# Two graph attention layers on one Trainium2 core: another order of the last pairs' work, and the bias product with its pieces side by side

## The chip, the core and the metric

The kernel runs on one core of one Trainium2 chip. A core has five engines that run side by side, each its own instructions in their order: TensorE (PE; its weight loads are the row PEld), VectorE (DVE), ScalarE (ACT), GpSimd (POOL) and SyncE (SP), which issues transfers. The metric is the device time of one execution in microseconds (us), lower is better.

## The reference

The input x has 64 graphs of 256 nodes with 512 features, float32, and one 256 x 256 adjacency matrix `adj` for all graphs. Two layers follow each other, each with a normalization, a ReLU and a residual:

```python
h = jnp.maximum(_layernorm(x, axis=-1), 0.0)
x = x + _L0_gnn_ref(h, adj, Wq, bq, Wk, bk, Wv, bv, Wo, bo)
h = jnp.maximum(_layernorm(x, axis=-1), 0.0)
x = x + _L1_gnn_ref(h, W, a, beta, adj)

# _L0_gnn_ref: 8 heads of 64
q, k, v = (h @ Wq + bq), (h @ Wk + bk), (h @ Wv + bv)        # as (b, n, 8, 64)
scores = einsum('bqhd,bkhd->bhqk', q, k) / 8 + (1 - adj) * -1e9
out = einsum('bhqk,bkhd->bqhd', softmax(scores), v)
return out @ Wo + bo

# _L1_gnn_ref
g = h @ W
e = leaky_relu((g @ a1)[:, :, None] + (g @ a2)[:, None, :], 0.2) * adj
return elu(softmax(e, axis=2) @ g + beta * g)
```

## The kernel before

The 64 graphs are worked on in 32 pairs. Each product with a weight matrix is one 2 x 2 block product: the two graphs of the pair are the rows, the two halves of the features the columns. It is done with seven block products in place of eight (a Strassen-like scheme), at the price of sums of blocks. A `Unit` is such a product for one pair: `UnitQK`, `UnitV`, `UnitO` (Wo) and `UnitW` (W of layer 1). Its method `p(i)` issues block product i on TensorE into the unit's PSUM banks `a`, `c` or `b`; for i = 1, 6, 7 ScalarE then copies bank `a` to SBUF (`u1`, `u2`, `u3`, line L278). `put11`, `put22`, `put21`, `put12` make the four result blocks from banks and copies. The blocks that go in are combined by `combine_31` (blocks 7 and 5), `combine_2` (block 6, L294) and `combine_4` (block 3, L298).

The order of every engine but SyncE is exactly the order in which the program is written (`tc.manual_schedule`), so where a call stands decides what an instruction queues behind. The stages of a pair p are: projections, scores and softmax (L416, L420, L421), `values` (L434, L443, L445), Wo with the residual (`UnitO`, L484 and L488), normalization of the result y (`y_stats`, `scales`, `normal`, L514), `node_sums` (L520; it is called by `y_sums`), `gat_scores` (L170, L530, L532), `gat_exp` (L537), `divide_1` (L542, L544), `gat_t` (four transposes on TensorE, L553, and a copy on ScalarE, L554), `z_graph` (L566, with copies on ScalarE, L569), and `UnitW`, whose blocks go through `elu` (ScalarE: L594, L595; VectorE: L599) and `finish` (POOL: L604; transfer out on SyncE: L605). Different pairs are in different stages at once. `first_half` and `second_half` do the steady state; `last` and `end` write out the order of the last two pairs, p - 1 and p. In `end`, `uv` is the `UnitW` of pair p - 2, `uw` that of pair p - 1 and then of pair p, `uo` the `UnitO` of pair p.

- `residual` (L466, L467) fetches a block of x and adds `bo2` on POOL; `o_blocks` makes two combined blocks on POOL (L459).
- `project_b` makes `bo2` = bo - 1 + bv Wo once, at the start. Its `part(0)` (called as `shift(0)`) spreads bv over 128 columns for each of four pieces of 128 rows (L191), `part(1)` multiplies them with Wo, adding the pieces up in PSUM (L197), and adds the result to `bo2` (L199). Its -1 belongs to elu.
- `in_range` (L726 to L728) looks on VectorE whether all softmax sums were in range; `count` adds the answer over partitions with one TensorE product (L733) and writes a flag, which decides whether a slow general version runs. With these inputs it does not.
- `p_34` does the last unit's products 3 and 4, and L632 and L636 add up the block of product 3 in its own bank; `put21_finish` makes the very last block in two halves (L645 to L651).

Tiles come from pools with a fixed number of buffers per tag (`BUFS`), and all PSUM tiles from 8 banks.

Of the kernel before, what the change touches and what calls it, by code (L numbers as in the profile page):

```python
# [11 lines left out]
ALU = mybir.AluOpType  # L12
# [11 lines left out]
def kernel(ctx: ExitStack, tc: tile.TileContext, x, adj, wq, bq, wk, bk, wv, bv, wo, bo, w, a, beta, out):  # L24
# [30 lines left out]
    def sb(shape, tag, name, bufs=2):  # L55
        return pools["sb"].tile(shape, F32, tag=tag, name=name, bufs=bufs)
# [3 lines left out]
    def blk(tag, name):  # L60

        return sb([P, 2, N], tag, name, BUFS[tag])
# [4 lines left out]
    def two(ps):  # L67
        return ps.rearrange("p (j n) -> p j n", j=2)
# [103 lines left out]
    def project_b():  # L172


        WO, b12, fetch, sums = weight("wo", wo, True)
        fetch(*range(4))
        nc.sync.dma_start(bo2, bo.partition_broadcast(P))
        bvc = sb([P, DC], "bvc", "bvc", 1)
        with nc.allow_non_contiguous_dma(reason="a bias, once"):
            bv_v = bv.rearrange("(q i s d) -> i d q s", q=2, i=4, s=2, d=HH)  # L180
            for i in range(4):
                for q in range(2):
                    nc.sync.dma_start(bvc[i * HH:(i + 1) * HH, 2 * q:2 * q + 2], bv_v[i, :, q, :])
        cbs = []

        def part(n):
            if n == 0:
                for c in range(DC):
                    if c % 2 == 0:
                        cbs.append(sb([P, 2, P], "rec", f"bvb_{c}"))  # L190
                    nc.vector.tensor_scalar(cbs[-1][:, c % 2, :], ones, bvc[:, c:c + 1], None, ALU.mult)  # L191
            else:
                ps = bank("pbo")
                for c in range(DC):
                    for f in range(2):
                        b = ((WO[1], b12), (WO[2], WO[3]))[c // 2][f]
                        nc.tensor.matmul(ps[:, f * N:(f + 1) * N], cbs[c // 2][:, c % 2, :], b[:, c % 2, :],  # L197
                                         start=(c == 0 and f == 0), stop=(c == DC - 1), skip_group_check=True)
                nc.vector.scalar_tensor_tensor(bo2, bo2, -1.0, ps, op0=ALU.add, op1=ALU.add)  # L199

        return WO, part, sums
# [79 lines left out]
        s = A[key] = {"name": name}  # L281
        return s

    def combine_31(s, a21, a22, tag="set"):

        s["tag"] = tag
        s[7] = blk(tag, f"s3_{s['name']}")
        a21(s[7], ALU.subtract, s[1])
        s[5] = s.pop("a21")
        a22(s[5], ALU.add, s[5])  # L290

# [158 lines left out]
            nc.vector.tensor_tensor(OT[b, q], two(ps), rec.unsqueeze(1).to_broadcast([P, 2, N]), ALU.mult)  # L450


    def o_blocks(p, tag="set"):
        s = blocks(("o", p), f"o{p}")
        for i, (gi, q) in zip(BLOCK, ((0, 0), (0, 1), (1, 0), (1, 1))):
            s[i] = OT.pop((2 * p + gi, q))

        def of(src):
            return lambda dst, op, other: nc.gpsimd.tensor_tensor(dst, src, other, op)  # L459

        combine_31(s, of(s["a21"]), of(s[4]), tag)

    def residual(p, gi, fh, tag):
        g = 2 * p + gi
# [119 lines left out]
    class UnitW(Unit):  # L584
# [41 lines left out]
            nc.vector.tensor_tensor(two(self.b), two(self.b), self.u2, ALU.add)  # L626
            self.elu(0, 1, two(self.b))

        def p_34(self):

            t = self.u2
            nc.vector.tensor_tensor(t, two(self.b), t, ALU.add)  # L632
            e = bank(f"{self.name}_p3")
            self.mm(3, e, True)
            self.p(4)
            nc.vector.tensor_tensor(two(e), two(e), t, ALU.add)  # L636
            self.elu(0, 1, two(e))

        def put21_finish(self):

            g = 2 * self.pair + 1
            y = Y.pop((g, 0))
            v, m, o = (blk("v", f"{c}_{g}_0") for c in "vmo")
            for t in range(NT):
                nc.vector.tensor_copy(v[:, t, :], self.a[:, t * N:(t + 1) * N])  # L645
                nc.scalar.activation(m[:, t, :], v[:, t, :], AF.Exp)
            for t in range(NT):
                nc.vector.scalar_tensor_tensor(o[:, t, :], v[:, t, :], 0.0, y[:, t, :], op0=ALU.max, op1=ALU.add)
            for t in range(NT):
                nc.vector.scalar_tensor_tensor(o[:, t, :], m[:, t, :], 1.0, o[:, t, :], op0=ALU.min, op1=ALU.add)  # L650
                nc.sync.dma_start(out[g, t * P:(t + 1) * P, :N], o[:, t, :])  # L651


    def products(u, *which):
# [59 lines left out]
    def combine_24(s):  # L714
        combine_2(s)
        combine_4(s)
# [22 lines left out]
    def start():  # L739
        warm = bank("warm")  # L740
        for i in range(32):
            nc.tensor.transpose(warm[:, i % 4 * P:(i % 4 + 1) * P], ident, ident)

        def normals(g):
            sc = []
            for t in range(NT):
                stats(f"x0{g}{t}", 1, 0, 0, XT[g, t])
                sc.append(scales(f"x0{g}{t}", 1))
            for t in range(NT):
                nmr = minus(sc[t][1], f"x0{g}{t}")  # L750
# [36 lines left out]
        products(uv, 2)  # L787
        products(ub, 3)
        scores(0)
        shift(0)  # L790
        prods, w_sums = project_a()
        products(uv, 6, 5, 7)
        prods(0)
        shift(1)
        products(uv, 4)
        x_t(1)
        load(2)
        products(uv, 3)
        combine_24(A["h", 1])
        return wo_blocks, (wo_sums, prods, w_sums)  # L800
# [117 lines left out]
    def last():  # L918
        p = NP - 1
        g0, g1 = 2 * p, 2 * p + 1  # L920
        uv = v_chain(p)
        gat_z(p - 2)
        o_blocks(p - 1, "x")
        residuals(p - 1, ALL, "qk")
        products(uv, 3)
        combine_24(A["z", p - 2])
        values(g0)
        scores(g1)
        combine_24(A["o", p - 1])
# [12 lines left out]
        y_normal(p - 1, 1)  # L942
        y_normal(p - 1, 0)
        values(g1)
        residuals(p, ALL[:2], "qk")
        o_blocks(p)
        residuals(p, ALL[2:], "qk")
        uw.p(5)
        y_sums(p - 1, 1, 0)
        uw.p(7)  # L950
        uo = UnitO(p)
        uo.p(1)
        combine_2(A["o", p])
        y_sums(p - 1, 1, 1)
        products(uo, 2)
        uo.p(6)
        gat_scores(g1 - 2)
        gat_exp(g1 - 2)
        uw.put22()
        combine_4(A["o", p])  # L960
        return uw, uo

    def end(uv, uo):
# [7 lines left out]
        y_stats(g1, NT, 0, g1, 1)  # L971
        uv.p(4)
        products(uo, 4)
        gat_scores(g0 - 2)
        y_stats(g1, NT, 0, g1, 0)
        rstd, mr = scales(f"y{g1}", 2)
        y_stats(g0, NT, 0, g0, 0)
        products(uo, 3)
        gat_t(g1 - 2)
        gat_exp(g0 - 2)  # L980
        divide_1(g0 - 2)
        y_stats(g0, NT, 0, g0, 1)
        rstd_0, mr_0 = scales(f"y{g0}", 2)
# [2 lines left out]
        gat_t(g0 - 2)  # L986
        uv.p(3)
        normal(g1, rstd, minus(mr, f"y{g1}"), "v")
        normal(g0, rstd_0, minus(mr_0, f"y{g0}"), "v")
        z_graph(p - 1, 0)  # L990
        z = A["z", p - 1]
        z["ps"] = ps
        z_31(p - 1)
# [22 lines left out]
        gat_t(g0)  # L1016
        uv.put21()
        uv.put12()
        uw.put11()
        uv.finish(1, 0, nc.gpsimd)  # L1020
        uv.finish(0, 1, nc.gpsimd)
        uw.p(3)
# [2 lines left out]
        A["z", p]["ps"] = ps  # L1025
        z_31(p)
        combine_24(A["z", p])
        uw.finish(0, 0, nc.gpsimd)
        uw.elu22()
        uw.put21()  # L1030
        uw.put12()
        uw.finish(1, 1, nc.gpsimd)
        uw.finish(1, 0, nc.gpsimd)
        uw.finish(0, 1, nc.gpsimd)
        uw = UnitW(p, "pt")
        products(uw, 1, 2)
        uw.p(6)
        uw.p(5)
        bad = in_range()
        uw.finish(0, 0, nc.gpsimd)  # L1040
        products(uw, 7)
        count(bad)
        uw.p_34()
        uw.finish(1, 1, nc.gpsimd)
        uw.finish(0, 1, nc.gpsimd)
        uw.put21_finish()
# [171 lines left out]
```

## Time and profile before

| | us |
|---|---|
| median of 3 runs | 2823.25 (2821.69 to 2823.27) |
| the profiled execution | 2823.8 |
| its span, first to last instruction | 2821.9 |
| last matmul group (products 3 and 4 of the last unit) | 2809.22 to about 2812.9 |
| last transfers issued | 2816.68 and 2817.1 |

| engine | busy us | share of the span |
|---|---|---|
| TensorE | 2802.0 | 99% |
| weight loads | 2346.4 | 83% |
| VectorE | 1909.3 | 68% |
| POOL | 1607.1 | 57% |
| ScalarE | 1208.7 | 43% |

Times in the profile are microseconds from the first instruction. A timeline line gives start, duration, engine, line of the program, operation, and how many instructions were merged into it; in brackets stands how long the engine was idle before it and what ended that. The duration of the last instruction of a group contains its latency, so the distance between starts is what a group occupies. One float32 product appears as two matmul instructions. A line of the waits gives who waited, for whom, and the total, the number and the longest of these waits in us.

### The profile page before, as it was taken

The numbers are of one execution on the slowest core, as the hardware profiler recorded it, in microseconds if no ns is written. First come the engines' busy times: TensorE is split into PE (matmuls) and PEld (weight loads), VectorE is DVE, ScalarE is ACT, GpSimd is POOL, SyncE is SP. The second block draws the span as 40 slices with busy tenths as digits, with TensorE's granted clock in tenths as the row PEclk, the third lists the DMA queues.
The fourth block names the chain that finished last, engine by engine and source line by source line (L and its number), as shares of the span: only waits on it lengthen the run. The fifth ranks groups of instructions, "written<-read, shape, count | busy, mean of one in ns | idle before, by whom it ended". The sixth has DMA issues, their size and how long they took to land.

```text
span 2821.9 us, 46417 instructions
## 1 busy us (share of the span) xinstructions
PE 2802.0 (99%) x18110; PEld 2346.4 (83%) x18110; DVE 1909.3 (68%) x3401; ACT 1208.7 (43%) x2438; POOL 1607.1 (57%) x1529
## 2 busy tenths in 40 slices
PE   9999999999999999999999999999999999999997
PEld 8888888888888888888888888888888888888876
DVE  6766766666766667676676666776666766667676
ACT  4343444344444434444344444444344444434434
POOL 4656546466464655656555556546465464655572
PEclk9999999999999999999999999999999999999999
DMA  5010011100111100111001110011110111101111
GB/s 152 6 45 23 23 46 45 46 27 27 38 46 46 35 27 31 46 46 46 16 31 46 46 46 23 23 46 46 46 30 24 38 46 46 38 23 31 38 31 46
DMA packets 96480, 110.01 MB, mean 39 GB/s; under 512 B 8576, under 2 KB 79488, under 8 KB 96256
## 3 DMA queue, kind: packets, MB, share of 16 engines
q1 hardware_dynamic: 96256, 106.99, 12.2%
q8 instruction: 145, 2.38, 0.3%
q14 instruction: 79, 0.65, 0.1%
HBM read 73.41 MB, written 33.55 MB: 38 GB/s over the span
## 4 chain that ended last, share of the span: by engine, by line


## 5 line engine op out<-in xcount | busy, mean ns | idle before, releaser
L421 POOL TENSOR_TENSOR pt<-pt,maskT 128x512 f32<-128x512 f32 x512 | 706.3, 1380 | 753.9 <-ACT pt L420 753.9
L420 ACT ACTIVATE pt<-sc 128x512 f32<-128x512 f32 x512 | 257.6, 624 | 452.3 <-PE sc L416 452.3
L423 POOL TENSOR_TENSOR pp<-pt 128x256 f32<-128x256 f32 x512 | 420.6, 822 | 40.2
L445 DVE RECIPROCAL rec<-sm 128x256 f32<-128x256 f32 x128 | 224.3, 1752 | 75.9 <-PE sm L443 75.9
L520 DVE SCALAR_TENSOR_TENSOR pr<-h,war 128x512 f32<-128x512 f32 x256 | 253.1, 1034 | 10.5 <-ACT h L514 10.5
L278 ACT COPY qk_u<-qk_p 128x512 f32<-128x512 f32 x192 | 112.0, 583 | 326.2 <-PE qk_p L346 323.5
L434 PE MATMUL av<-pt,v 128*32 128x256 f32 x4096 | 246.0, 380 | 0.0
L416 PE MATMUL sc<-qk 64*128 64x256 f32 x2048 | 238.5, 383 | 0.0
L359 DVE SCALAR_TENSOR_TENSOR qk<-qk_p,bq,qk_u 128x256 f32<-128x256 f32 x192 | 90.8, 473 | 212.2 <-ACT qk_u L278 192.0
L416 PEld LDWEIGHTS sc<-qk 64*128 64x128 f32 x2048 | 193.0, 187 | 46.0 <-issue 13.9
L566 PE MATMUL pz<-eT,h 128*128 128x256 f32 x1024 | 226.7, 379 | 0.7 <-ACT eT L554 0.7
L566 PEld LDWEIGHTS pz<-eT,h 128*128 128x128 f32 x1024 | 194.5, 190 | 27.3 <-ACT eT L554 0.9
L434 PEld LDWEIGHTS av<-pt,v 128*32 128x32 f32 x4096 | 126.6, 110 | 98.1 <-issue 21.2
L467 POOL TENSOR_TENSOR y<-y,bo 128x512 f32<-128x512 f32 x128 | 174.3, 1373 | 33.3 <-DVE y L488 19.8
L580 DVE TENSOR_TENSOR s_z<-pz,z 128x512 f32<-128x512 f32 x32 | 22.1, 692 | 220.5 <-ACT z L569 220.5
L484 POOL TENSOR_TENSOR y<-y,o_u 128x512 f32<-128x512 f32 x60 | 101.1, 1685 | 79.9 <-ACT o_u L278 79.8
L544 DVE SCALAR_TENSOR_TENSOR e<-e,grec,betai 128x256 f32<-128x256 f32 x128 | 134.9, 1093 | 2.3
L569 ACT COPY z<-pz 128x512 f32<-128x512 f32 x128 | 74.9, 586 | 140.8 <-PE pz L566 140.8
L346 PE MATMUL qk_p<-h,wq_b 128*128 128x256 f32 x512 | 134.7, 386 | 0.2 <-ACT h L323 0.2
L514 ACT ACTIVATE h<-y,nmr_y,rstd_y 128x256 f32<-128x256 f32 x256 | 132.8, 590 | 1.1
L604 POOL TENSOR_TENSOR o<-o,m 128x512 f32<-128x512 f32 x29 | 36.8, 1270 | 167.9 <-DVE o L599 167.9
L346 PE MATMUL qk_p<-h,wq_t 128*128 128x256 f32 x512 | 131.4, 379 | 0.0
(159 smaller groups left out, 6173.0 us busy)
## 6 DMA issues: line engine op xcount, KB each, us to landing
x<-in_x_dram SPq DMA_DIRECT2D x128, 256.0 KB, 2.8
y<-in_x_dram SPq DMA_DIRECT2D x128, 256.0 KB, 2.8
out_dram<-o SPq DMA_DIRECT2D x116, 256.0 KB, 2.2
out_dram<-y SPq DMA_DIRECT2D x11, 256.0 KB, 2.1
wq_b<-in_L_gnn_Wq_dram SPq DMA_DIRECT2D x4, 256.0 KB, 5.8
wk_b<-in_L_gnn_Wk_dram SPq DMA_DIRECT2D x4, 256.0 KB, 6.1
wv_b<-in_L_gnn_Wv_dram SPq DMA_DIRECT2D x4, 256.0 KB, 5.0
wo_b<-in_L_gnn_Wo_dram SPq DMA_DIRECT2D x16, 64.0 KB, 2.4
```

The source lines that it names most:

```text
L346: nc.tensor.matmul(ps[:, j * N:(j + 1) * N], wj[i][:, c, ft * P:(ft + 1) * P], s[i][:, c, :], start=(start and j == 0 and c == 0), stop=(c ...
L416: nc.tensor.matmul(pss[2 * pair + h][:, k * N:(k + 1) * N], qk[hs, 1, k * P:(k + 1) * P], qk[hs, 0, :], start=True, stop=True)
L420: nc.scalar.activation(pt, two(pss[i]), AF.Exp, scale=QSCALE)
L421: nc.gpsimd.tensor_tensor(pt, pt, maskT, ALU.mult)
L423: nc.gpsimd.tensor_tensor(pp, pt[:, 0, :], pt[:, 1, :], ALU.add)
L434: nc.tensor.matmul(ps[i * HH:(i + 1) * HH, s * N:(s + 1) * N], v[:, k, c0:c0 + HH], pts[i][:, k, :], start=(k == 0), stop=(k == NT - 1))
L445: nc.vector.reciprocal(rec, sums[:, :N])
L467: nc.gpsimd.tensor_tensor(r, r, bo2[:, fh * N:(fh + 1) * N].unsqueeze(1).to_broadcast([P, 2, N]), ALU.add)
L514: nc.scalar.activation(h2[t][:, f * N:(f + 1) * N], Y[g, f][:, t, :], AF.Relu, bias=nmr[:, t:t + 1], scale=rstd[:, t:t + 1])
L520: nc.vector.scalar_tensor_tensor(pr, H2[g][t], 1.0, war[:, j, :], op0=ALU.mult, op1=ALU.mult, accum_out=SC[g][:, t, j:j + 1])
L544: nc.vector.scalar_tensor_tensor(e[:, t, :], e[:, t, :], rec[:, t:t + 1], betai[:, (1 - t) * P:(3 - t) * P], op0=ALU.mult, op1=ALU.add)
L566: nc.tensor.matmul(ps[:, f * N:(f + 1) * N], h2[k][:, fs], eT[:, k, :], start=(k == 0), stop=(k == NT - 1))
```

## The change

- `project_b`: `part(0)` spreads bv over 32 columns instead of 128. `part(1)` multiplies the four pieces into four strips of 32 rows of one bank, side by side, and ScalarE copies the bank. A new `part(2)`, called after the next pair's loads, adds the strips with `pick`, a matrix that has ones in one row of each strip, and then adds to `bo2`.
- `last`: one of the four residuals of the last pair is added on POOL between the two operations of `o_blocks`.
- `end`: `gat_t(g1 - 2)` and `gat_exp(g0 - 2)` stand earlier, and `z_graph(p - 1, 0)` stands before the normalization of g0.
- `end`, last two units: the first product of the last unit, with its copy, stands ahead of the elu blocks of the unit before; the rest of both is interleaved. `put11` of the unit before moves behind `z_graph(p, 0)`. The sum of bank `b` and `u2` (L632) moves ahead, out of `p_34`.
- `put21_finish` takes its tiles from another tag, and issues the last transfer from ScalarE instead of SyncE.

```diff
@@ project_b
         cbs = []
+        pick = blk("c", "pick")[:, 0, :P]
+        nc.gpsimd.memset(pick, 0.0)
+        for i in range(4):
+            nc.gpsimd.memset(pick[i * HH:i * HH + 1, :], 1.0)
...
-                    if c % 2 == 0:
-                        cbs.append(sb([P, 2, P], "rec", f"bvb_{c}"))
-                    nc.vector.tensor_scalar(cbs[-1][:, c % 2, :], ones, bvc[:, c:c + 1], None, ALU.mult)
+                    if c == 0:
+                        cbs.append(sb([P, DC, HH], "rec", "bvb"))
+                    nc.vector.tensor_scalar(cbs[0][:, c, :], ones[:, :HH], bvc[:, c:c + 1], None, ALU.mult)
+            elif n == 1:
+                ps = bank("pbo_c")
+                for f in range(2):
+                    for c in range(DC):
+                        b = ((WO[1], b12), (WO[2], WO[3]))[c // 2][f]
+                        nc.tensor.matmul(ps[c * HH:(c + 1) * HH, f * N:(f + 1) * N], cbs[0][:, c, :],
+                                         b[:, c % 2, :], start=True, stop=True)
+                cbs.append(blk("c", "pbo_s"))
+                nc.scalar.copy(cbs[1], two(ps))
             else:
                 ps = bank("pbo")
-                for c in range(DC):
-                    for f in range(2):
-                        b = ((WO[1], b12), (WO[2], WO[3]))[c // 2][f]
-                        nc.tensor.matmul(ps[:, f * N:(f + 1) * N], cbs[c // 2][:, c % 2, :], b[:, c % 2, :],
-                                         start=(c == 0 and f == 0), stop=(c == DC - 1), skip_group_check=True)
+                for f in range(2):
+                    nc.tensor.matmul(ps[:, f * N:(f + 1) * N], pick, cbs[1][:, f, :], start=True, stop=True)
                 nc.vector.scalar_tensor_tensor(bo2, bo2, -1.0, ps, op0=ALU.add, op1=ALU.add)
@@ combine_31, called by o_blocks with between
         a21(s[7], ALU.subtract, s[1])
+        between()
         s[5] = s.pop("a21")
         a22(s[5], ALU.add, s[5])
@@ p_34
-        def p_34(self):
-            t = self.u2
-            nc.vector.tensor_tensor(t, two(self.b), t, ALU.add)
+        def p_34(self, t):
@@ put21_finish
-            v, m, o = (blk("v", f"{c}_{g}_0") for c in "vmo")
+            v, m, o = (blk("qk", f"{c}_{g}_0") for c in "vmo")
...
-                nc.sync.dma_start(out[g, t * P:(t + 1) * P, :N], o[:, t, :])
+                (nc.sync, nc.scalar)[t].dma_start(out[g, t * P:(t + 1) * P, :N], o[:, t, :])
@@ start
         load(2)
+        shift(2)
         products(uv, 3)
@@ last
-        o_blocks(p)
-        residuals(p, ALL[2:], "qk")
+        o_blocks(p, "set", lambda: residuals(p, ALL[2:3], "qk"))
+        residuals(p, ALL[3:], "qk")
@@ end
         products(uo, 4)
+        gat_t(g1 - 2)
         gat_scores(g0 - 2)
+        gat_exp(g0 - 2)
         y_stats(g1, NT, 0, g1, 0)
...
         products(uo, 3)
-        gat_t(g1 - 2)
-        gat_exp(g0 - 2)
         divide_1(g0 - 2)
...
         normal(g1, rstd, minus(mr, f"y{g1}"), "v")
+        z_graph(p - 1, 0)
         normal(g0, rstd_0, minus(mr_0, f"y{g0}"), "v")
-        z_graph(p - 1, 0)
...
         uv.put12()
-        uw.put11()
         uv.finish(1, 0, nc.gpsimd)
         uv.finish(0, 1, nc.gpsimd)
         uw.p(3)
...
         combine_24(A["z", p])
+        uv, uw = uw, UnitW(p, "pt")
+        uw.p(1)
+        uv.put11()
+        uv.elu22()
+        uv.finish(0, 0, nc.gpsimd)
+        uv.finish(1, 1, nc.gpsimd)
+        uw.p(2)
+        uw.p(6)
+        uv.put21()
+        uv.finish(1, 0, nc.gpsimd)
+        uw.p(5)
+        t = blk("v", "u2_p5")
+        nc.vector.tensor_tensor(t, two(uw.b), uw.u2, ALU.add)
+        uv.put12()
+        uv.finish(0, 1, nc.gpsimd)
+        uw.put11()
         uw.finish(0, 0, nc.gpsimd)
-        uw.elu22()
-        uw.put21()
-        uw.put12()
-        uw.finish(1, 1, nc.gpsimd)
-        uw.finish(1, 0, nc.gpsimd)
-        uw.finish(0, 1, nc.gpsimd)
-        uw = UnitW(p, "pt")
-        products(uw, 1, 2)
-        uw.p(6)
-        uw.p(5)
         bad = in_range()
-        uw.finish(0, 0, nc.gpsimd)
         products(uw, 7)
         count(bad)
-        uw.p_34()
+        uw.p_34(t)
```

More of the change, by code (lines that the diff above doesn't have):

```diff
@@ L282, in blocks, with combine_31 @@
         return s
-    def combine_31(s, a21, a22, tag="set"):
+    def combine_31(s, a21, a22, tag="set", between=lambda: None):
         s["tag"] = tag
@@ L450, in values, with o_blocks @@
             nc.vector.tensor_tensor(OT[b, q], two(ps), rec.unsqueeze(1).to_broadcast([P, 2, N]), ALU.mult)
-    def o_blocks(p, tag="set"):
+    def o_blocks(p, tag="set", between=lambda: None):
         s = blocks(("o", p), f"o{p}")
@@ L459, in of @@
             return lambda dst, op, other: nc.gpsimd.tensor_tensor(dst, src, other, op)
-        combine_31(s, of(s["a21"]), of(s[4]), tag)
+        combine_31(s, of(s["a21"]), of(s[4]), tag, between)
     def residual(p, gi, fh, tag):
```

## The prediction

> **What bounds the kernel now.** I read the page first: TensorE is busy for 99% of the span, so only its own work, or its idle time, can be taken away.
>
> ```profile
> PE 2802.0 (99%) x18110; PEld 2346.4 (83%) x18110; DVE 1909.3 (68%) x3401; ACT 1208.7 (43%) x2438; POOL 1607.1 (57%) x1529
> ```
>
> Then the table of stretches (busy us of each engine, granted clock, DMA share) and TensorE's waits over the end. Up to 2740 TensorE does not stop; from there it does. In 2740:2760 VectorE has 19.79 of 20 us: it sets the pace there.
>
> ```profile
> 2720.00:2740.00 20.00, 20.00 (x145) 16.35 (x147) 13.08 (x24) 5.46 (x11) 16.64 (x19) 1.00 0.06 20
> 2740.00:2760.00 20.00, 17.90 (x97) 14.33 (x86) 19.79 (x37) 7.34 (x17) 10.69 (x7) 1.00 0.00 1
> ...
> 2800.00:2810.00 10.00, 7.96 (x30) 6.45 (x31) 4.81 (x12) 4.10 (x7) 4.18 (x4) 0.83 0.31 105
> 2810.00:2822.00 12.00, 2.94 (x14) 2.25 (x12) 6.09 (x13) 3.24 (x6) 2.53 (x2) 0.78 0.22 70
> ```
>
> ```profile
> PE w_p L381 <- ACT w_u L278: 2.7, 1, 2.7
> PE pe L170 <- DVE pr L520: 1.9, 2, 1.2
> PE w_p L381 <- ACT z L569: 1.6, 2, 1.2
> PE pz L566 <- ACT eT L554: 0.7, 1, 0.7
> ```
>
> All waits there come to 7.7 us; what the end can give is that, plus the half-rate stretch after the 2.7 us wait, plus part of the 9 us behind the last matmul. Last, the timelines, for durations. A product of `mm` is 8 matmul instructions, 1.73 us from start to start (2753.63 to 2755.36).
>
> **a) bv Wo.** TensorE at the start, in order of time:
>
> ```profile
> 47.40 3.62 PE L197 MATMUL pbo<-wo_b,bvb 128*128 128x256 f32 x16
> 50.85 1.89 PE L381 MATMUL v_p<-wv_t,h 128*128 128x256 f32 x8
> ...
> 56.15 1.93 PE L434 MATMUL av<-pt,v 128*32 128x256 f32 x32
> 57.90 0.61 PE L443 MATMUL sm<-pp,ones 128*32 128x256 f32 x8
> ```
>
> Now: 50.85 - 47.40 = 3.45 us. Afterwards 16 instructions of 32 columns; L434 has that shape, 32 in 57.90 - 56.15 = 1.75 us, so 0.87; about 0.1 for each change between 128 and 32 columns (the product at 54.33 takes 1.82 before L434, not 1.73), so 0.2; and `pick`'s two products, 4 x 0.216 = 0.86. Sum 1.93, saving 1.5. Bounds: a loss of 0.9 if the strips did not overlap, a gain of 1.7 if nothing were lost in changing; I take L434's. The rest is covered: five memsets fall into POOL's 21.56 us of idle before 33.12 (a 128x128 one took 0.20); ScalarE's copy (0.59) into its 4.59 us before 52.78; VectorE's four broadcasts shrink. The add to `bo2` moves behind x_31, and POOL reads `bo2` only after scores(1). Without cover each would cost its own duration. TensorE then comes 1.5 earlier to the second L434 group (58.33, so 56.8), whose last masked block POOL ends at 56.32: 0.5 us of slack. **1.5 us**, carried through, as TensorE has no wait up to 2740.
>
> **b) The residual inside o_blocks.** POOL and VectorE, same stretch:
>
> ```profile
> 2744.53 1.58 POOL L459 TENSOR_TENSOR oT<-oT,oT 128x512 f32<-128x512 f32 x1 [1.46 <-DVE oT L450]
> ...
> 2746.07 3.39 POOL L467 TENSOR_TENSOR y<-y,bo 128x512 f32<-128x512 f32 x2
> ...
> 2748.26 1.75 DVE L520 SCALAR_TENSOR_TENSOR pr<-h,war 128x512 f32<-128x512 f32 x1
> 2749.42 3.39 POOL L484 TENSOR_TENSOR y<-y,o_u 128x512 f32<-128x512 f32 x2
> ```
>
> L520 takes 0.68 at 2744.30 and 1.75 while POOL runs: the two take turns. L488, with an operand in PSUM, takes 0.68 under POOL's L484. The moved L467 (1.27) fills POOL's idle 1.46, so s5 stays, the second L467 ends at 2747.77, and the first L484 ends where L467 did, 2749.46. The L520 of 2748.26 ends as before; the next (2749.94) finds POOL idle: 0.61 instead of 1.67. It releases TensorE 1.06 sooner (the 1.19 wait at 2751.74). But the second L484 still waits for u2's copy (2751.07), runs to 2752.39, and now covers L532, which starts at 2752.04 and ends near 2752.95 instead of 2753.71. VectorE, without a gap until 2767, keeps **0.75** (between 0 and 1.06). The transfers keep their order on SP; (1,0)'s data has been there since about 2722.
>
> **c) gat_t and gat_exp earlier.** The four transposes (0.44) go into the gap before uo.p3 (p4 ends at 2758.8, p3 waits for L495 until 2759.83), and the 0.67 wait for eT goes: z_graph(p-1,1) moves from 2762.93 to 2760.8. The next transposes, however, wait for divide_1(g0-2), at the end of VectorE's full row (2766.49, now 2765.73). TensorE waits 1.5 us there instead: **0** beyond b.
>
> **d) z_graph(p-1,0) before normal(g0).** ScalarE's copies of z no longer stand behind normal(g0) (2770.11 to 2772.18). The first falls at 2769.8; L580 and the four L520 start 2.2 earlier, and the 0.43 and 0.67 waits before p1 and before the scores' transposes go. normal(g0) now ends at 2774.4, then u1's copy: p6 at 2775.1 instead of 2777.36. With b, **2.3** in sum, and z_graph(p,0) moves from 2790.84 to 2788.55. Cover: ScalarE is idle 3.88 us before 2779.20; without it normal(g0)'s 2.3 us would be back. Its readers, the L520 of g0, come at 2776.8.
>
> **e) The last two units.** Before:
>
> ```profile
> 2801.42 0.57 ACT L278 COPY w_u<-w_p 128x512 f32<-128x512 f32 x1
> ...
> 2802.03 2.76 PE L381 MATMUL w_p<-w_t,s_z 128*128 128x256 f32 x8 [2.70 <-ACT w_u L278]
> ...
> 2806.38 0.17 DVE L728 TENSOR_SCALAR bad<-bad 128x3 f32<-128x3 f32 x1
> ...
> 2809.10 0.19 PE L733 MATMUL count<-bad,ones 128*1 128x3 f32 x2
> ...
> 2816.68 2.12 SPq L651 DMA_DIRECT2D out_dram<-o  x2
> ```
>
> The finishes keep their order on POOL and their transfers theirs on SP. With z_graph(p,0) at 2788.55: z copies 2790.8 and 2792.2 (put11's 0.6 + 0.6 is off ScalarE), p1 at 2792.0 (2795.61 before), u1's copy at 2793.95, p2 2793.7, p6 2795.45, p5 2797.2, p7 2798.9 to 2800.6 without a wait. But in_range now stands behind put11, elu22, put21, t, put12 and the unit's put11 on VectorE. Each sum in PSUM is a round trip: VectorE to ScalarE 0.74 (2799.53 to 2800.25), then L599 only after L594, 0.63. Chain: L608 2794.1, L594 2794.85, 2795.48, 2796.0, 2796.65; u2's copy 2797.4; put21 2797.95, its L599 2798.6; t 2799.2; L626 2799.8, L594 2800.5, L599 2801.2; L608 2801.8, L594 2802.5, L599 3.15; in_range 2803.76 against 2803.99, its end 2806.3 against 2806.55 (again held up by POOL's finish). `count` waits for it, and mm3 and p4 stand behind `count` on TensorE, which is idle from 2800.6 to 2806.4. mm3 starts at 2806.5 (2809.22 before). With t already added: L636 2808.5, L594 2809.3, L599 2809.9, copies 2810.5, POOL's finish until 2812.0, last sums 2812.55, transfer 2813.0 instead of 2816.68: 3.7, of which 2.3 is from above: **1.4**.
>
> Against this stands the clock:
>
> ```profile
> 2803.00:2806.00 3.00, 3.00 (x9) 2.37 (x8) 2.55 (x6) 1.56 (x3) 1.27 (x1) 0.52 0.37 127
> ```
>
> After 2.70 us of idle the clock is half for 3.4 us. By that row alone, the new 5.8 us wait costs 1.7 in mm3 and p4. The Trainium skill, "TensorE: Matmul & The Clock Gate", section "What's actually happening", has a free-running window of about 3.4 us: half rate after an idle window, full after a busy one. (Our 2.70 us sufficed, so a window need not be empty.) By the rule the half rate lasts until the first busy window ends, at any phase: 1 to 4.5 us, costing 0.5 to 2.2. I take **-1.3**.
>
> **f) Last transfers.** v, m, o in `qk`: those blocks have been sent by 2808, so nothing. Before, the second L651 issue took 1.68, the first 0.34, and they land 3.4 to 3.5 us after. By that row a queue of its own might save 1.3; by the skill's "DMA: Bandwidth & Descriptors", section "Issuing engines are not separate DMA queues", only the sequencer's issuing time is saved, for the same 16 engines carry both. No row shows a transfer issued by ScalarE; bounds -0.5 (an issue slower than SP's) to 1.3. I take **0.1**.
>
> **Sum.** 1.5 + 2.3 + 1.4 - 1.3 + 0.1 = 4.0. The profiled execution took 2823.8 (span 2821.9), 0.55 over the median of 2823.25; so 2819.8 for such an execution, and 2819.3 as a median.
>
> **Rivals.** *More comes out* (0.25): the restart falls well in the window (0.5 instead of 1.3), L532 escapes POOL (+0.3), the second issue's 1.68 was queueing (+1.2): 6.3, 2816.9. For it: the row of the second issue; against: the windows at 2816:2818 show engines moving bytes at 139 and 254 GB/s. *The end gives nothing* (0.17): VectorE's full row absorbs b and d, the half rate takes 1.9: 1.5 + 1.4 + 0.1 - 1.9 = 1.1, 2822.1. For it: 19.79 of 20 us; against: the two waits of d are ScalarE's order, not VectorE's load. *Slower* (0.03): the chain from L608 to in_range has seven VectorE instructions, with POOL's finishes beside them. If POOL held each up by 1.06, as it does L520, in_range ends 7.4 later and the kernel takes 2826.7; from four held up it is slower than now. Against: L599 and L626 have operands in PSUM, and L599 takes 0.69 under POOL's finishes at 2800.88. *The change as described fails*: the copy goes ahead of the elu blocks, but TensorE waits as long, for `count`; that is in the forecast.
>
> **How the numbers follow.** The likeliest case (0.55) is the sum. About 0.2%, 5.6 us, is what a measurement of this kernel can tell from no change, so faster means below 2817.6: that is the first rival, 0.25. Slower by as much needs the third and more, 0.03. The rest, 0.72, is within. The range 2816.6 to 2822.1 reaches from the first rival to the second.
>
> **What would show it.** Right: L197 in two pieces of about 0.9 us each; the wait of w_p for w_u (2.7) gone; a wait of about 1.5 at the transposes near 2765; p1 near 2790.5 on the new span (2792.0 - 1.5); TensorE idle for about 5.8 us before `count`, with the clock at 0.5 behind it; in_range nearly where it was, less 1.5. Wrong: no idle before `count` (the gain is then larger), L520 still at 1.75 near 2750, or VectorE instructions of over 1 us at 2795 to 2803.

## The result, and the profile after

| | before | after |
|---|---|---|
| median, us | 2823.26 (2821.69 to 2824.0, 20 runs) | 2818.68 (2818.4 to 2819.08, 20 runs) |
| profiled execution, its span | 2823.8, 2821.9 | 2818.67, 2816.9 |
| ratio | | 0.9984, 95% interval 0.9978 to 0.9991 |

The kernel is 4.6 us faster in the medians, 0.16%; the forecast was 4.0, with 2819.3 as the new median. The spans of the two profiled executions lie 5.0 apart. Line numbers shift: L381 becomes L393, L520 L532, L566 L578, L553 L565, L617 L629, L651 L661, L733 L743.

TensorE's row of the page after; the four instructions more are the products of `pick`:

```profile
PE 2801.0 (99%) x18114; PEld 2345.3 (83%) x18114; DVE 1921.1 (68%) x3401; ACT 1208.8 (43%) x2439; POOL 1602.4 (57%) x1534
```

Its waits (who waited <- for whom, total, number, longest), and the table of stretches:

```profile
PE count L743 <- DVE bad L738: 5.4, 1, 5.4
PE at L565 <- DVE e L556: 0.9, 1, 0.9
PE o_p L393 <- DVE s_o L306: 0.5, 1, 0.5
...
2740.00:2760.00 20.00, 19.09 (x90) 15.91 (x89) 19.79 (x38) 6.71 (x15) 8.70 (x7) 1.00 0.00 0
...
2800.00:2805.00 5.00, 0.00 (x0) 0.00 (x0) 4.20 (x11) 2.22 (x4) 2.52 (x2) 0.68 0.33 112
2805.00:2817.00 12.00, 5.52 (x18) 4.27 (x18) 5.59 (x13) 3.21 (x6) 2.53 (x2) 0.78 0.27 89
```

The four waits of before are gone from the list's head. One takes their place: 5.4 us for `bad`. In 2740:2760 TensorE is busy 1.2 us longer, with VectorE as full as before.

The start, in order of time:

```profile
47.43 1.07 PE L202 MATMUL pbo_c<-wo_b,bvb 128*32 128x256 f32 x16
...
48.44 1.99 PE L393 MATMUL v_p<-wv_t,h 128*128 128x256 f32 x8
...
52.01 1.03 PE L209 MATMUL pbo<-pbo_s,pick 128*128 128x256 f32 x4
52.88 1.89 PE L393 MATMUL v_p<-wv_b,s_h 128*128 128x256 f32 x8
54.70 1.93 PE L446 MATMUL av<-pt,v 128*32 128x256 f32 x32
```

The strips take 48.44 - 47.43 = 1.01, `pick` 0.87; L446 starts at 54.70 instead of 56.15.

VectorE and POOL around the moved residual:

```profile
2744.86 1.72 POOL L479 TENSOR_TENSOR y<-y,bo 128x512 f32<-128x512 f32 x1
...
2746.53 1.71 POOL L496 TENSOR_TENSOR y<-y,o_u 128x512 f32<-128x512 f32 x1
...
2748.72 0.68 DVE L532 SCALAR_TENSOR_TENSOR pr<-h,war 128x512 f32<-128x512 f32 x1
...
2749.99 1.27 POOL L496 TENSOR_TENSOR y<-y,o_u 128x512 f32<-128x512 f32 x1 [1.75 <-ACT o_u L289]
2750.83 0.98 DVE L544 SCALAR_TENSOR_TENSOR e<-e 128x512 f32<-128x512 f32 x1
2751.73 0.68 DVE L629 TENSOR_TENSOR o<-w_p,w_u 128x512 f32<-128x512 f32 x1
```

The fourth L532 takes 0.68, not 1.74. L544 pays 0.29 of that back, since POOL's second L496 now lies over it. L629 stands at 2751.73, before at 2753.71: 1.98 sooner, 1.22 of it from the start.

The tail, SyncE and ScalarE as issuers included:

```profile
2802.91 1.12 DVE L736 TENSOR_SCALAR ok<-gsums 128x128 f32<-128x128 f32 x1
...
2804.84 0.17 DVE L738 TENSOR_SCALAR bad<-bad 128x3 f32<-128x3 f32 x1
...
2805.07 0.19 PE L743 MATMUL count<-bad,ones 128*1 128x3 f32 x2 [5.45 <-DVE bad L738]
2805.19 3.67 PE L393 MATMUL w_p<-w_b,s_z 128*128 128x256 f32 x8
...
2808.70 1.89 PE L393 MATMUL w_p<-w_t,z 128*128 128x256 f32 x8
...
2813.41 0.34 SPq L661 DMA_DIRECT2D out_dram<-o  x1
2813.75 0.38 ACTq L661 DMA_DIRECT2D out_dram<-o  x1
```

Product 3 takes 3.51 us from start to start, twice its 1.73. Its clock, by stretches:

```profile
2798.50:2801.90 3.40, 1.12 (x6) 0.64 (x4) 2.07 (x5) 1.87 (x4) 2.10 (x2) 0.98 0.45 154
2801.90:2808.60 6.70, 3.53 (x10) 2.87 (x11) 4.46 (x12) 2.32 (x4) 2.62 (x3) 0.50 0.24 81
2808.60:2812.00 3.40, 1.99 (x9) 1.41 (x8) 2.38 (x5) 1.80 (x4) 0.84 (x1) 1.00 0.26 82
```

Half the rate from 2801.9 to 2808.6: 6.8 us, two stretches as long as the one of before (2803.1 to 2806.5, 3.4).

The last transfers are issued at 2813.41 instead of 2816.68, 3.27 sooner; the span is shorter by 5.0. The rest is behind the issue. The last transfers' time to landing, before (L651) and after (L661):

```profile
DMA to landing us min/median/max: 3.4/3.5/3.5
```

```profile
DMA to landing us min/median/max: 1.7/1.7/1.8
```

The queues' packets, MB and share in the time of those transfers, 2816.68 to 2820.6 before, then 2813.4 to 2815.6 after:

```profile
q1 hardware_dynamic: 550, 0.51, 38.8%
q8 instruction: 1, 0.02, 2.5%
q14 instruction: 1, 0.01, 0.9%
```

```profile
q1 hardware_dynamic: 402, 0.38, 51.9%
q10 hardware_dynamic: 144, 0.13, 17.7%
q14 instruction: 1, 0.01, 1.1%
```

The bytes are the same, 0.51 MB: the two last transfers and, as in all traces here, one of 256 KB that was issued 0.95 us ahead of them. Before, a fetch of instructions (queue q8, one packet of 16 KB, 2816.85 for 1.59 us) lies on the last transfers. After, it comes at 2811.65 for 1.47 us and is over before they are issued.

The account of the 5.0: 1.2 from the start (2740.82 to 2739.60), 2.25 between 2740 and `z_graph(p, 0)` (2790.84 to 2787.37, less the 1.2), -0.2 in the tail up to the first last transfer, 0.1 because the second follows by 0.34 instead of 0.44, and 1.7 from the landing (3.42 to 1.76).

### The profile page after: what moved, and what is told of

Its sections match the earlier page's. It is cut to its first block, busy times and chain, and to the rows that moved or that the text cites. A ratio compares the mean times of both kernels' runs of the same rounds, so it can differ in the third digit from the quotient of the medians.

```text
span 2816.9 us, 46430 instructions
## 1 busy us (share of the span) xinstructions
PE 2801.0 (99%) x18114; PEld 2345.3 (83%) x18114; DVE 1921.1 (68%) x3401; ACT 1208.8 (43%) x2439; POOL 1602.4 (57%) x1534
## 4 chain that ended last, share of the span: by engine, by line
## 5 line engine op out<-in xcount | busy, mean ns | idle before, releaser
L532 DVE SCALAR_TENSOR_TENSOR pr<-h,war 128x512 f32<-128x512 f32 x256 | 260.7, 1063 | 10.6 <-ACT h L526 10.6
L446 PE MATMUL av<-pt,v 128*32 128x256 f32 x4096 | 246.0, 380 | 0.0
L578 PE MATMUL pz<-eT,h 128*128 128x256 f32 x1024 | 226.6, 379 | 0.0
L578 PEld LDWEIGHTS pz<-eT,h 128*128 128x128 f32 x1024 | 194.6, 190 | 26.4
L446 PEld LDWEIGHTS av<-pt,v 128*32 128x32 f32 x4096 | 126.6, 110 | 98.1 <-issue 20.9
L496 POOL TENSOR_TENSOR y<-y,o_u 128x512 f32<-128x512 f32 x60 | 100.3, 1671 | 86.7 <-ACT o_u L289 86.7
```

The costliest lines, as they stand in the source:

```text
L446: nc.tensor.matmul(ps[i * HH:(i + 1) * HH, s * N:(s + 1) * N], v[:, k, c0:c0 + HH], pts[i][:, k, :], start=(k == 0), stop=(k == NT - 1))
L532: nc.vector.scalar_tensor_tensor(pr, H2[g][t], 1.0, war[:, j, :], op0=ALU.mult, op1=ALU.mult, accum_out=SC[g][:, t, j:j + 1])
L578: nc.tensor.matmul(ps[:, f * N:(f + 1) * N], h2[k][:, fs], eT[:, k, :], start=(k == 0), stop=(k == NT - 1))
```

## The experiments

**Each part by itself.** `f_only`: the kernel before, with the last transfer issued from ScalarE.

```diff
-                nc.sync.dma_start(out[g, t * P:(t + 1) * P, :N], o[:, t, :])
+                (nc.sync, nc.scalar)[t].dma_start(out[g, t * P:(t + 1) * P, :N], o[:, t, :])
```

> The kernel before with one edit: the last transfer is issued by ScalarE instead of SyncE. Before, the two last transfers landed 3.4 to 3.5 us after their issue and the second issue took 1.68 us; after, 1.7 to 1.8 us and 0.38. Theory Q (the queue: the second transfer stood behind the first on SyncE's queue): the end of the kernel comes 1.3 to 1.6 us earlier, 2821.8. Theory I (an instruction fetch of 16 KB on another queue was under way from 2816.85 for 1.59 us and held both transfers up, whoever issues them): the last transfers still land some 3.4 us after their issue, and the time is that of before, 2823.2, less 0.1.

Measured: 2822.01 (2821.41 to 2823.69), ratio 0.9999 (0.9991 to 1.0007). The second issue costs 0.38 instead of 1.68, and the landing stays at 3.1 to 3.2 us, with a 16 KB fetch (2814.67 to 2816.0) on top of it. Its times are of two kinds, 2821.4 to 2822.0 and 2822.8 to 2823.7, and so are those of before: of 49 executions measured beside this kernel, 19 took 2821.3 to 2822.2 and 30 took 2822.8 to 2825.0. So the median of 2822.01 is no gain over the 2823.2 of before: 7 of its 13 executions are of the short kind. Kind against kind the medians are 2821.8 against 2821.7 and 2823.2 against 2823.4. The issue's 1.68 was no queueing that a queue of its own takes away from the end. The profiled execution of `f_only` is one of the short kind, and in it the products behind the 2.70 us wait run at full rate:

```profile
2801.91 1.99 PE L381 MATMUL w_p<-w_t,s_z 128*128 128x256 f32 x8 [2.70 <-ACT w_u L278]
2803.74 1.89 PE L381 MATMUL w_p<-w_t,z 128*128 128x256 f32 x8
```

`after_sp`: the same line the other way round, in the changed kernel.

```diff
-                (nc.sync, nc.scalar)[t].dma_start(out[g, t * P:(t + 1) * P, :N], o[:, t, :])
+                nc.sync.dma_start(out[g, t * P:(t + 1) * P, :N], o[:, t, :])
```

> The kernel after, with its last transfer issued by SyncE again. Theory Q: 1.3 to 1.6 us are lost, 2820.1, and the second issue takes about 1.7 us again. Theory I: the fetch of 16 KB now runs from 2811.65, ahead of the last transfers, so they land in 1.8 us whoever issues them: 2818.8, at most 0.2 more than after.

Measured: 2819.03 (2818.46 to 2819.68), 0.9986 (0.998 to 0.9993); landing 1.9. The queue is worth 0.35 at most, and the short landing does not come from it.

`a_only`: the kernel before with the two edits of `project_b` and the call of `shift(2)` alone.

```diff
         products(uv, 4)
         x_t(1)
         load(2)
+        shift(2)
         products(uv, 3)
```

> The kernel before with the bv Wo part alone (strips side by side, pick, the part called after the loads). Predicted saving 1.5; the trace of after has 1.39 at 59.15 and 1.22 at 2739.60. If the saving is carried through to the end: 2821.8 to 2822.1 against 2823.26. If the end is set by something that TensorE's earlier start does not move: 2823.2. The position of the instruction fetch against the last transfers moves too, so the end may differ by up to 1.5 from the place of the last product: the product p4 of the last unit should start at 2809.8 in the span (2811.05 before).

Measured: 2821.83 (2820.28 to 2822.47), 0.9996 (0.9987 to 1.0004), again of two kinds, 2820.3 to 2820.7 and 2821.8 to 2822.5. Kind against kind that is 1.0 and 1.2 us less than before. In the traces the first scores start at 60.39 to 60.60 in four executions with the old `project_b` and at 59.00 to 59.26 in ten with the new one, 1.4 sooner on average; at 2740, where it is used, 1.25 of that is left (2740.70 to 2740.83, against 2739.43 to 2739.62). Most of the 0.15 in between is lost at once, behind the first scores. From their start to the next projection TensorE takes 3.65 us in the four old executions and 3.77 to 3.80 in the ten new ones. In all ten that projection starts 0.05 us after the same VectorE instruction ends (L459 in the changed kernel, at 62.88):

```profile
62.93 0.73 PEld L358 LDWEIGHTS qk_p<-h,wq_b 128*128 128x128 f32 x4 [0.39 <-DVE sm L459]
```

VectorE is only 0.8 earlier there (62.88 instead of 63.68), so TensorE, which came 1.45 earlier, runs into it and waits some 0.13 us.

`e_only`: the kernel before with the new order of the last two units, `t` and the `qk` tiles; `project_b`, `last`, the first part of `end` and the issuing engine as before.

```diff
+        uv, uw = uw, UnitW(p, "pt")
+        uw.p(1)
+        uv.put11()
+        uv.elu22()
...
+        uw.put11()
+        uw.finish(0, 0, nc.gpsimd)
         products(uw, 7)
         count(bad)
-        uw.p_34()
+        uw.p_34(t)
```

> The kernel before with the order of the last two units alone (copies ahead of the elu blocks, put11 moved, the sum of bank b and u2 ahead, tiles of the last block from the other tag), last transfer still from SyncE. Theory of the prediction: TensorE reaches count early and waits some 5 to 6 us for in_range, which is hardly earlier than before (2806.1 against 2803.99 to start, as the two other gains are missing); mm3 at 2808.8 against 2809.22, then at half rate: gain 1.4 less 0.5 to 1.9, so 2821.9 to 2823.8. Rival (copies ahead bring what the removed wait of 2.7 us and the half rate of 1.7 cost): 4 us faster, 2819.2.

Measured: 2822.61 (2822.36 to 2823.01), of one kind only; 1.0 (0.9992 to 1.0008).

```profile
2808.48 0.19 PE L731 MATMUL count<-bad,ones 128*1 128x3 f32 x2 [5.45 <-DVE bad L726]
2808.60 3.78 PE L381 MATMUL w_p<-w_b,s_z 128*128 128x256 f32 x8
```

The wait for `bad` and the half rate are there without any other part. The last transfers go out at 2816.93, 0.25 later than before: the new order by itself gains nothing up to that point. They land in 2.1 to 2.2 us, with the fetch at 2814.88, ahead of them; that 1.3 us is all that it saves against the long kind of before. Against the short kind, 2821.7, it is 0.9 slower.

**Parts taken out of the changed kernel.** `no_c`: `gat_t(g1 - 2)` and `gat_exp(g0 - 2)` back behind `products(uo, 3)`.

```diff
         products(uo, 4)
-        gat_t(g1 - 2)
         gat_scores(g0 - 2)
-        gat_exp(g0 - 2)
...
         products(uo, 3)
+        gat_t(g1 - 2)
+        gat_exp(g0 - 2)
         divide_1(g0 - 2)
```

> The kernel after with gat_t(g1 - 2) and gat_exp(g0 - 2) where they were before. The prediction has nothing for this move: the 0.9 us that TensorE waits at the next transposes would swallow its 0.44 + 0.67. So 2818.7, within 0.3. Rival (the move is worth its 1.1 us): 2819.8.

Measured: 2818.68 (2818.24 to 2819.11), 0.9985 (0.9978 to 0.9991), the changed kernel's own median. The part is worth nothing. The timelines tell why, as the prediction had it. In `no_c` `z_graph(p - 1, 1)` waits for eT, and the transposes behind it wait for nothing; in the changed kernel (the second pair of lines) it comes sooner, but the transposes wait for divide_1, and the product behind them starts no sooner (2764.95, in `no_c` 2764.83):

```profile
2760.84 3.72 PE L578 MATMUL pz<-eT,h 128*128 128x256 f32 x16 [0.68 <-ACT eT L566]
2764.40 0.60 PE L565 MATMUL at<-ident,e 128*128 128x128 f32 x4
```

```profile
2759.68 3.62 PE L578 MATMUL pz<-eT,h 128*128 128x256 f32 x16
...
2764.17 0.94 PE L565 MATMUL at<-ident,e 128*128 128x128 f32 x4 [0.87 <-DVE e L556]
```

`no_b`: the residual back behind `o_blocks`.

```diff
-        o_blocks(p, "set", lambda: residuals(p, ALL[2:3], "qk"))
-        residuals(p, ALL[3:], "qk")
+        o_blocks(p)
+        residuals(p, ALL[2:], "qk")
```

> The changed kernel with part b undone: the residual (1,0) of the last pair stands again behind both operations of o_blocks, not between them. Theory (the step of the prediction, 0.75 us, carried through to the end): L629's counterpart near 2752.5 instead of 2751.73, z_graph(p,0) near 2788.1 instead of 2787.37, 2819.4 us in all. Rival 1 (the whole 1.06 us of the L532 that ran beside POOL counts): 2819.7. Rival 2 (what b gives is taken up by a later wait, so it is worth nothing): 2818.7. All three hold if the last transfers land in 1.8 us as in the changed kernel; if the instruction fetch falls on them, 1.3 to 1.7 us more.

Measured: 2819.5 (2819.09 to 2819.82), 0.9988 (0.9981 to 0.9995): 0.8 more than the changed kernel. `z_graph(p, 0)` starts at 2788.13, 0.76 later, and lands as the changed kernel does (1.7 to 1.8). VectorE's two lines:

```profile
2748.72 1.74 DVE L532 SCALAR_TENSOR_TENSOR pr<-h,war 128x512 f32<-128x512 f32 x1
...
2752.50 0.68 DVE L629 TENSOR_TENSOR o<-w_p,w_u 128x512 f32<-128x512 f32 x1
```

L532 ends 1.06 later, L629 starts 0.77 later: the first expectation, not the whole 1.06.

`no_d`: `z_graph(p - 1, 0)` back behind the normalization of g0.

```diff
         normal(g1, rstd, minus(mr, f"y{g1}"), "v")
-        z_graph(p - 1, 0)
         normal(g0, rstd_0, minus(mr_0, f"y{g0}"), "v")
+        z_graph(p - 1, 0)
```

> The changed kernel with part d undone: z_graph(p-1,0) stands again behind the normalization of g0. Theory (prediction: 2.3 for b and d together, 0.75 of it b): p6 of the unit p-1 and z_graph(p,0) 1.5 us later (2788.9 instead of 2787.37), 2820.2 us in all. Rival (the two copies of z would have come free anyway, since VectorE sets the pace there): no change, 2818.7. Here too 1.3 to 1.7 us more if the instruction fetch falls on the last transfers.

Measured: 2820.25 (2819.91 to 2820.36), 0.9991 (0.9983 to 1.0): 1.6 more than the changed kernel. TensorE's waits show two of before again, which the changed kernel does not have:

```profile
PE pe L170 <- DVE pr L532: 0.7, 1, 0.7
...
PE w_p L393 <- ACT z L581: 0.4, 1, 0.4
```

p6 starts at 2775.17 instead of 2773.90, `z_graph(p, 0)` at 2788.64, 1.27 later, although this execution was 0.16 ahead at 2740 (2739.44 against 2739.60): d is worth 1.43 there. VectorE's full row before it does not swallow the gain.

**The clock and the fetch.** `warm`: the changed kernel with 46 transposes of the identity into a bank that nobody reads, ahead of `count`, which fill TensorE's idle time.

```diff
+        keep = bank("keep")
+        for i in range(46):
+            nc.tensor.transpose(keep[:, i % 4 * P:(i % 4 + 1) * P], ident, ident)
         count(bad)
```

> The kernel after, with 46 transposes of a constant into an unused bank between p7 and count, 4.9 us of the 5.45 us in which TensorE waits for in_range. They add nothing to the results and end before bad is there. Theory of the clock: TensorE no longer falls to half rate, mm3 takes 1.73 instead of 3.51, and everything behind it comes 1.8 us earlier: 2816.9. Rival (the half rate is beside the path, and the sums on VectorE and ScalarE set the end): 2818.7, no change. If the instruction fetch comes to lie on the last transfers again, up to 1.6 of it is lost.

Measured: 2818.42 (2817.58 to 2818.92), 0.9984 (0.9978 to 0.9991), only 0.26 less than the changed kernel. In the trace, though:

```profile
2805.22 1.99 PE L393 MATMUL w_p<-w_b,s_z 128*128 128x256 f32 x8
...
2811.75 0.34 SPq L661 DMA_DIRECT2D out_dram<-o  x1
```

Product 3 starts when it did and runs at full rate, and the last transfers go out 1.66 sooner. They land in 3.2 to 3.4 us instead of 1.7 to 1.8: the fetch stays at 2811.62 (1.44 us) and now lies on them. The half rate costs 1.66 us in front of the transfers, and in this kernel the fetch takes that back.

`before_warm`: the kernel before with 22 such transposes in the 2.7 us wait ahead of p6.

```diff
+        keep = bank("keep")
+        for i in range(22):
+            nc.tensor.transpose(keep[:, i % 4 * P:(i % 4 + 1) * P], ident, ident)
         uw.p(6)
```

> The kernel before with 22 transposes of a constant into an unused bank in the 2.7 us wait before p6 of the last unit (2.35 us of it). They add nothing to the results. Theory of the clock: the kernel before takes one of two times, 2823.4 with the half rate after that wait and 2821.5 without, by where the clock's window falls; with TensorE kept busy only 2821.5 is left. Rival (the two times are of another cause, such as the landing of the last transfers): both stay.

Measured: 2821.71 (2821.46 to 2821.98), 0.9996 (0.9988 to 1.0004). The 13 times are all of the short kind of before; the long kind is gone. So the two kinds are the clock: after a wait of 2.70 us the half rate comes in some executions and not in others. It takes 3.4 us when it comes and costs half of that, 1.7, which is the distance of the kinds (2821.7 and 2823.4). How much TensorE worked in the 3.41 us just ahead of the half rate goes with it: 1.08 us in before and 0.77 in `a_only`, which then fell to half rate, while in `f_only`, which did not, no such stretch around the wait has less than 1.74. (Where `f_only`'s stretches begin is an estimate: steps of 3.41 us back from its next change of clock, at 2813.89.)

**A better version.** `early`: the changed kernel with in_range behind the last sum22 of the unit p - 1 and `count` behind its product 3, where the sums that in_range reads have long been there.

```diff
         uw.p(4)
         uw.sum22()
+        bad = in_range()
         z_graph(p, 1)
...
         uw.p(3)
+        count(bad)
         ps = A["z", p]["ps"]
...
-        bad = in_range()
         products(uw, 7)
-        count(bad)
         uw.p_34(t)
```

> The kernel after, with in_range put on VectorE behind sum22 of pair p - 1 (where VectorE is idle for 2.7 us and POOL for 18 us), and count behind p(3) of that unit. Theory (count's wait for in_range is what holds the end): mm3 follows p7 at once, p4 waits only for u3's copy, in_range's 2.5 us go out of the chain on VectorE, no half rate: the last transfer is issued near 2808.8 instead of 2813.4, 2814.1 in all (up to 2815.7 if the fetch falls on the last transfers). Rival (the chain of sums through PSUM sets the end anyway): not more than the 2.5 us of in_range less what the sums take in its place, 2817.

Measured: 2815.97 (2815.59 to 2816.73), 0.9975 (0.9965 to 0.9985). Product 3 of the last unit starts at 2800.17, straight behind product 7, there is no half rate, and the last transfers go out at 2809.63, 3.8 sooner than in the changed kernel. That is 0.8 later than expected, and they land in 3.4 to 3.6 us with the fetch (2810.19) on them. Two waits are left: product 4's 1.7 for `u3`, and, in the weight loads of `z_graph(p, 0)`,

```profile
2789.70 1.59 PEld L578 LDWEIGHTS pz<-eT,h 128*128 128x128 f32 x8 [0.43 <-DVE count_f L745]
```

`early2`: `count` behind product 5 of the last unit.

```diff
         uw.p(3)
-        count(bad)
...
         uw.p(5)
+        count(bad)
         t = blk("v", "u2_p5")
```

> The earlier in_range (behind sum22 of the unit p-1) with count placed behind block product 5 of the last unit instead of behind product 3 of the unit before. Theory (in the earlier version, z_graph(p,0)'s second half waited 0.43 us for the add of count, whose bank it needed; that is what made the first product of the last unit 0.7 us late): no such wait, p1 at 2790.8 instead of 2791.53, last transfers near 2809.0, 2815.3 us. Rival (the 0.7 us is VectorE's six instructions of in_range themselves, which stand ahead of the elu blocks and of z's sums wherever count is): p1 at 2791.5, 2816.0 us.

Measured: 2815.4 (2814.65 to 2816.03), 0.9975 (0.9965 to 0.9985). That wait is gone and p1 starts at 2790.65 instead of 2791.53: it was `count`'s place, not the load of in_range on VectorE.

`early3`: as `early2`, and product 7 of the last unit ahead of put11.

```diff
+        uw.p(7)
         uw.put11()
         uw.finish(0, 0, nc.gpsimd)
-        products(uw, 7)
+        uw.put22()
```

> As early2, and the block product 7 of the last unit with its copy (u3) stands ahead of put11 of that unit, so that ScalarE copies u3 at about 2800 instead of 2803.1. Theory (p4's wait of 1.7 us for u3 is the last idle time of TensorE, and the tail hangs on p4): p4 follows product 3 at once, near 2801.3, and the last transfers come up to 1.7 us sooner than in early2: 2813.6 us. Rival (without that wait the tail hangs on ScalarE and POOL, which still have put11, put22 and put12 of the last unit in front of the last block: 3 x 1.27 us of ScalarE and the finishes of 1.27 on POOL): at most 0.5 us sooner, 2814.8 to 2815.3 us.

Measured: 2814.61 (2814.47 to 2814.72), 0.9971 (0.9961 to 0.9982), the fastest of all: 4.1 below the changed kernel. But not as the first expectation had it:

```profile
2801.46 1.89 PE L393 MATMUL w_p<-w_t,z 128*128 128x256 f32 x8
...
2809.23 0.34 SPq L661 DMA_DIRECT2D out_dram<-o  x1
```

Product 4 comes 1.7 sooner (2803.18 in `early2`), and the last transfers do not (2809.10 there): as the rival said, the tail hangs on the elu blocks of ScalarE and VectorE by then. What is gained is the landing, 1.8 instead of 3.4 to 3.5: the fetch came at 2806.68, ahead of the last transfers, in `early2` at 2809.32, on top of them. Between the two profiled executions that makes 1.4 us, between the medians 0.8; the profiled one of `early2` was its slowest.

## Why the prediction was right, and where it was not

The total held, 4.6 against 4.0, and the mechanisms of a to e are those that it named. The rivals do not describe what happened: neither did the end give nothing, nor did seven VectorE instructions hold up in_range. One sign listed against the forecast did appear, a VectorE instruction of over 1 us ahead of 2803 (L736, 1.12 at 2802.91). It belongs to in_range itself, and it took 1.12 before as well, so it cost nothing new. But two terms of the sum were mis-sized and one was missing, and they cancelled in part. That the total came so near is partly luck: up to the issue of the last transfers the change gave 3.3 us, and 1.7 of the 5.0 between the profiled executions came from a place that the forecast had at nothing.

- **a**, forecast 1.5. At its own place the step is right: 1.01 + 0.87 for the products and L446 1.45 sooner. What counts at 2740 is 1.25. "Carried through, as TensorE has no wait up to 2740" is the phrase that failed: none was there before, but the earlier start made one, 0.13 us for VectorE at 62.93, and the step had looked only at POOL's slack at the second L434 group.
- **b**, 0.75: `no_b` measured 0.76 by the trace, 0.82 by the medians. That L544 and L629 would stand under POOL's second addition is what the trace shows.
- **c**, 0: `no_c` measured 0.0. The new wait was 0.87 rather than 1.5.
- **b to d**, 2.3: 2.25 by the trace; `no_d` gives 1.43 by the trace and 1.57 by the medians for d alone, where 1.5 was left for it.
- **e**, 1.4 without the clock: product 3 starts at 2805.19. in_range starts at 2802.46; the prediction's 2803.76, less 1.25 for a, is 2802.5. `warm`, which has the new order without the half rate, sends the last block 4.93 sooner than before (2816.68 to 2811.75); less 1.25 and 2.25, that is 1.43. `e_only` agrees: its last transfers go out 0.25 later than before, and 1.43 less the 1.66 of the next term is -0.23.
- **The clock**, forecast -1.3: `warm` measured 1.66. The term was the middle between ends; here all of product 3 ran at half rate. The rule of the Trainium skill, "TensorE: Matmul & The Clock Gate", section "What's actually happening", fits this: the half rate is two stretches of 3.4 us; the first, to 2805.2, has TensorE busy for 0.13 us, the second is busy and still at half rate, and behind it the clock is full. The row alone would have given 1.7. All six traces with this wait (the changed kernel, `after_sp`, `e_only`, `no_b`, `no_c`, `no_d`) have the two stretches, 6.83 us, though not at the same phase: the half rate begins 1.1 (`no_b`) to 3.4 us ahead of `count` and ends 3.4 to 5.7 behind it, where the forecast had 1 to 4.5. In `no_b` even a stretch with TensorE busy for 2.30 of 3.41 us did not end it. In all six it covers the whole of product 3 or all but 0.1 us of it; where it went on over product 4 it cost little, as `no_b` sends its last transfers only 0.88 later than the changed kernel, of which 0.76 are b. That fits the changed kernel's 20 times, which lie within 0.7 us. No trace shows a wait of 5.45 us that escaped.
- **f**, 0.1: at most 0.35 by `after_sp`, nothing clear by `f_only`. The 1.3 of the issue row was not there to be had; the section "Issuing engines are not separate DMA queues" of "DMA: Bandwidth & Descriptors", which the prediction weighed against that row, was the better guide.
- **Missing: the landing.** 1.7 us of the 5.0 between the spans come after the last issue. The prediction read "they land 3.4 to 3.5 us after" as the price of the transfers; it was the price of the transfers with a fetch on them. All fourteen traces read the same way: 1.7 to 2.2 where the fetch lies ahead (the changed kernel, `after_sp`, `no_c`, `no_b`, `no_d`, `e_only`, `early3`), 3.0 to 3.6 where it lies on them (before, `f_only`, `warm`, `early`, `early2`, `before_warm`). In `a_only` the transfer under the fetch took 3.3, and the second, issued 0.5 us after the fetch had ended, 2.3. That the fetch is the cause rests on this agreement alone: no run moved the fetch and nothing else.

What sets the fetch's moment can be read from the traces. Queue q8 seems to be TensorE's: in the kernel before it brings 145 packets of 16 KB, one for about 250 of TensorE's matmuls and weight loads, and no other engine keeps so even a count. At the end its packets follow TensorE's branch on the flag that `count` makes possible, before and after:

```profile
L1169 PEldq COMPARE_BRANCH  x1: 3955/3955/3955, 2812.1 to 2812.1; - x1
```

```profile
L1184 PEldq COMPARE_BRANCH  x1: 3715/3715/3715, 2807.2 to 2807.2; - x1
```

In all fourteen traces one packet comes 1.0 to 1.8 us after this branch starts, and a second, the one that matters here, 4.1 to 5.7 us after it. What counts is thus how long the branch starts ahead of the last transfers: 4.5 to 5.1 us in the seven traces that met the fetch, 6.1 to 7.3 in the seven that did not. It also explains two runs. In `warm` the transfers came 1.66 sooner and the branch did not (2807.23), since the flag was made no sooner. In `early3` product 4, and with it the branch, came sooner than in `early2` (2801.97, not 2803.99), and the transfers did not. So the changed kernel was spared the fetch because its branch came 4.9 us sooner and its last transfers only 3.3; nothing in the change was meant for that.

By the sums: 1.25 + 2.25 + 1.43 - 1.66 + 0.1 + 1.7 = 5.07, against 5.03 between the landings of the profiled executions. (This sum has to close, as 1.43 and 1.66 are both taken from `warm`'s trace; `no_b`, `no_d` and `e_only` are the independent tests of the terms.) In the medians it is 0.5 less, because the profiled execution of before was long by 0.55, as the prediction allowed for.

One more thing was not seen: before has two kinds of executions, 1.7 apart, and its median is of the long kind. Against the short kind, 2821.7, the change brings some 3 us, not 4.6.

## What to carry to other kernels

A check that nobody waits for should be issued where its inputs are ready and where its engine has room, not where it happens to be finished: here one product for a flag held up TensorE for 5.45 us and then ran its successor at half rate, and moving it, with product 7, was worth another 4.1 us. Before a tail is costed, look at what else the queues carry while the last transfers land: their time to landing may not be theirs. Here a fetch came 4.1 to 5.7 us after a branch of TensorE, and the landing was short only where the last transfers came later still. And when a step ahead takes a wait away, ask which engine's order gives the next one: b and d shortened the path and came out to 0.1 us, c only moved a wait, and **a** lost 0.13 us to an engine that had not come forward as far as TensorE.

## What was not expected of the hardware

- A fetch of instructions, 16 KB in one packet on a queue of its own, went with last transfers of 128 KB each that took 3.0 to 3.6 us to land in place of 1.7 to 2.2. It came 4.1 to 5.7 us after TensorE's branch at the end, in all fourteen traces.
- The same wait of 2.70 us brought half the clock in some executions of one kernel and not in others, for 3.4 us, and made two times of 2821.7 and 2823.4 of it; a wait of 5.45 us brought it for 6.8 us in all six traces that have such a wait.
- A 128x128 VectorE comparison, 0.22 us, took 1.12 beside POOL's addition (L736, one of three in in_range), as the larger L532 takes 1.75 in place of 0.68.
